# A first and a last group of half the size in a Mamba and dense mixture-of-experts kernel, with the order of its first turns written anew

## The chip, the cores and the metric

The kernel runs on one core of one Trainium2 chip. The core has a matrix engine (PE), a vector engine (DVE), a scalar engine for activations (ACT), a general engine (POOL) and a queue that issues transfers (SP). The time is the device time of one execution in microseconds (us). Before the change it is 934.35 us, the median of three runs (933.2 to 934.37).

## What is computed

Sixteen sequences of 256 tokens, each token a row of 128 numbers, pass through one Mamba block with a small feed-forward network behind it, and then through eight experts of which every one is applied to every token. All numbers are 32-bit floats. Cut to what matters:

```python
# per sequence; D_INNER = 256 (two halves of 128), D_STATE = 16
xi, z = split(layernorm(x, ln1) @ in_proj_w.T)
xc    = silu(causal_conv4(xi) + conv_b)
dt, B, C = split(xc @ x_proj_w.T)                 # 8, 16, 16 columns
dt    = softplus(dt @ dt_proj_w.T + dt_b)
h_t   = exp(dt * A) * h_{t-1} + dt * B * xc        # for each of 256 channels and 16 states
y     = (sum over states of C * h) + D * xc
x1    = x + (y * silu(z)) @ out_proj_w.T
x1    = x1 + relu(layernorm(x1, ln2) @ w1.T + b1) @ w2.T + b2
x2    = layernorm(x + x1)
out   = layernorm(x2 + sum_e (silu(x2 @ Wg[e]) * (x2 @ Wu[e])) @ Wd[e])
```

## The kernel before

**Groups.** The sixteen sequences are taken in groups, `GROUPS = (2,) * 8`: eight groups of two sequences, so 512 token columns each. Channels lie on the 128 partitions, tokens along the free dimension. `W[g]` is the width of a group in columns, `NJ[g]` its number of expert slices; for 512 columns it is 32, one slice for each of 8 experts and 4 blocks of 128 hidden units.

**What one group passes through.** `stage_a` (L339) normalises, transposes, projects (`pi`, L430), convolves on DVE (L443), makes `dt`, `B` and `C` (`pd`, `pv`), writes B and C to DRAM (`bc`, L380, issued by ACT), takes the softplus and forms `u = dt * xc` (L402, on POOL but for one half of group 0). `stage_gate` (L412) makes the gate `zg`. The scan has 32 steps per group, one for each state and each half of the channels. A step is made of: `decay` (L466), an exponential on ACT that writes the factor `dA` into one of `ND` = 3 PSUM banks; `inject` (L479), the product `dBx = B * u` on POOL; `step` (L488), the scan on DVE (L494) and the product `hC` with C (L497), on DVE or, where the order says `p`, on POOL; and `add_state` (L505), which adds `hC` to the sum over states, on POOL (`y`, L523), or, where the order says `e`, on PE into the bank `py` (L521) by a product with the identity. B and C come back from DRAM spread over the partitions by `fetch` (L458), in tiles of two states, two buffers of each, issued by SP. When the last state is added, `yt` is formed (L536) and `stage_c` (L543) follows: the output projection `po` (L551), the sum with x (L558), a normalisation, the feed-forward network `pf` and `pff` (L595, L585), the residual sum `res` (L565, L566, on POOL), a second normalisation, and the transposed result `x2T`. Then the group's expert slices can be worked: `up` (L637) is the product `pg` and its silu, `across` (L646) the product `pu` and the product of both on DVE (L651), `down` (L654) the accumulation `acc` (L667). `stage_e` (L672) closes the group and writes the output. A group of one sequence is handled by the same code: `parts` (L632) puts two (expert, block) pairs of 256 columns into one slice, and `sums` (L499) puts both channel halves into one bank.

**The order.** Nothing is scheduled by a planner at build time: `tc.manual_schedule()` keeps the order in which the code issues instructions, and each engine works its own queue in that order. The order comes from strings of letters. PRE is worked once, then one string of START for each of the first 18 turns, then the 8 strings of TURN over and over. Every letter calls one function, if its condition allows it: L fetches B and C, `s` and `p` are a scan step with the product on DVE or on POOL, `a` and `e` an addition on POOL or PE, `i` inject, `d` decay, `u`, `x`, `w` one slice of up, across, down, and A, B, G, P, C, Z move the running stages by half a step. `m` issues four transposes of the identity into a bank that nothing reads (`busy`, L770), before any expert slice exists.

**Banks and silus.** Four PSUM banks (`NB`) are shared by stages and slices. A stage that takes a bank (`take`, L305) waits in its own program order until fewer than `limit[0]` are held by stages; the limit is `HELD` = (3, 1): three while no slice is ready, one while slices are. Likewise stages that need a silu or softplus on ACT wait, while slices are ready, for the stretch between the letters S and E (`silu_time`, L331).

**Weights.** Before PRE, SP issues the loads of `NEARLY` = 4 experts (L255, three loads of 256 KB for each). The others follow at the beginning of turns 1 to 4 (L799).

**The end.** For the last group `down` splits the accumulation into two parts (`NTAIL` = 2), and holds the last four slices back, so that the two closing stages follow one another.

Of the kernel before, what the change touches and what calls it, by code (L numbers as in the profile page):

```python
# [12 lines left out]
P = 128  # L13
L = 256
# [4 lines left out]
ROW = 32  # L19
KC = 4  # L20
TB = 512
GROUPS = (2,) * 8
NTT = TB // P
NE = 8
NF = 4
# [7 lines left out]
NLATE = 4  # L33
NTAIL = 2
BUFS = 6
HELD = (3, 1)
NB = 4
NEARLY = 4
EPS = 1e-5
FAR = 1e28  # L40
SLOW = 1e-25
# [7 lines left out]


PRE = (
    "L A B A G A L B A G B A A B G m G G A P L L B A A B B L B B "
    "B L P B d d B G B B B A P A A P B G G B L A m L s P d L B L "
    "G A P B A L L L A B A P A A L m i A G A A i G P P G i i G A "
    "B A B A m G m"
)
START = (
    "C i C L L Z m e e a L d C Z p s C s A Z m L s m A s Z i s i "
    "s e",
    "i d e Z A e A A s d s e L C i L Z C m C e A i Z m",  # L60
    "A e C C A i s C C A A C m a Z C e L C d A d A A i A C C e d "
    "e A C L Z A L C s A C",
    "L e d C C Z e e Z A m L d s A Z e s d i i A C C a C s Z A i "
    "L A i i p C d s A s i C L A A d A",
    "L s Z s A m C i L i p s C A i e d d m C L m Z i A L m C C s "
    "i m d d L L L L Z A C C A A e e A C i A C p C e A e m Z C C "
    "Z i",
    "p A A C A A L s C Z d i A d e C d i A C C e A A A A C L i L "
    "A m Z C e e A i L C A C A e m Z a i m C p m s Z m",
    "C s d A A d m A A Z m A i A i i s Z a C L C L m s e C d L A "  # L70
    "Z L C s a C Z L L s A C m L a",
    "A C L d e e e A A m C C a Z A e d i C d i A A C L A A L s e "
    "L C e Z C C A e L s i C L i C m d A d A d C L",
    "L s d A d Z C d C A C s i Z d L i a A d d A d a Z d A A C i "
    "d s A Z L A i C A L i d d C C p C C s C A i C d m C A d A A "
    "C A Z C i L Z a s d Z d i m A",
    "d e C A A p i C p A C s e d L C A A s m L A L a d C C A Z p "
    "C d Z C A A Z m s C L m C Z m Z a d A C C m i d a C",
    "p L A i Z C Z Z s u C i i C Z C p u Z C e x d A i L C x L C "
    "d x C e A C A w p E A C i d i C d Z C w A Z x i C C A Z w S "  # L80
    "C a u C s C C u C L",
    "u d p C w C a C C C C C x i u C m C Z a x p m L C C i i m C "
    "C C w p m C m C x Z i i d i s x E a d C d S Z a u w C L i C "
    "A i",
    "w p u w E p A u Z C m A L A C s C m a S A p Z L s C C d A s "
    "u C A s x m x u A L e s e A m a d A d x A x m A p Z i Z Z A "
    "A w w a d p C A w i C C i",
    "Z x C u w S A m A w Z Z e C s w Z e A A C i w i C s u i A i "
    "u u C L A x A d A Z C x Z L p m L p A A x L C a x Z w A A C "
    "A d C p E C C i",  # L90
    "L L u x Z C A Z C C s u p p i C x C d A Z e u L A w A C d A "
    "L A s C i w e A m A d A C C d C m a C d C Z i L x w C Z C u "
    "s Z w C a C Z C",
    "s i C a i u L w C A L u d L L i S i C A C C x A u A m e i i "
    "C x C e x w m A s C A a u d L C i i w u C A",
    "C s S L e a w a p u i A x A w A A a C C C d Z m u A x d x C "
    "x S C d p C w p E E A x C p Z C A w A A d A C d i Z C Z Z C "
    "m C A d d A C u C S C A C C m C i A m",
    "w C E A C A i A Z C L i C p C A m A w s u u C u x Z w x x a "
    "i d a Z p u w x C A d C L d C i s m E d a C Z L w a i L L A "  # L100
    "u L A",
)
TURN = (
    "w A C Z C s C s i C i Z x C C u s L a u L Z A C x C A A x C "
    "Z Z d C C C C C Z d C a C C w C E d C C L w C w s C A x C d "
    "u L C C C a Z d C C i C u",
    "C u A i w S s u s C i A C a d a Z E Z d A a A x C d C Z a w "
    "C C i C Z A A s C C S C u Z Z x s C C x a d a Z d w d i C A "
    "x d",
    "w u A a s u C C C s C E C L s w A C A u i C a x C A C C A A "  # L110
    "A Z L C C C A S C x w A a C C x C C i C A A S C A i s A Z C "
    "d i E A i C Z C Z i A Z x u C C Z u C Z A C w C A A C",
    "A w C A A a s s C x Z d C A A a d C u w C C a C u w u A E A "
    "A A Z A C a C a i Z s x x L i s s C Z L C u C A Z A C C A x "
    "C w A C A C C C A w A Z A C A C x d L C s C C w Z C a",
    "d s A C A d C u L A C w u C A a x x C A C C a C C x C d A d "
    "C C C s A u i i i A C A",
    "C w C C S a C A x C C u A a A A u s i w s d L w S A a C Z s "
    "C x C C s C C A a C A i a x i d A C A Z A E L L C A w u A C "
    "d",  # L120
    "C A a S C u C S Z u w C w C a A A w s x i u A C C i A u A C "
    "x Z s A A i Z Z C C d a Z x A E A A w L s x C x C A d w s a "
    "w i L C C C i d d C C Z i C i C C a i C d",
    "s A E s C d d Z C u s Z A u C d w s C a C u i x C a A u A w "
    "C x x w A C u d x C w C i A i C C L C u",
)


# [1 line left out]
def kernel(  # L130
# [25 lines left out]
    nc = tc.nc  # L156
    NG = len(GROUPS)
    W = [n * L for n in GROUPS]
    NJ = [NE * NF * w // TB for w in W]
# [12 lines left out]
    def bank(tag, name, bufs=1, w=TB):  # L172
        return ps.tile([P, TB], FP, tag=tag, bufs=bufs, name=name)[:, :w]
# [76 lines left out]
    def load_expert(e):  # L250
        nc.sync.dma_start(out=wg[:, e, :], in_=Wg[e])
        nc.sync.dma_start(out=wu[:, e, :], in_=Wu[e])
        nc.sync.dma_start(out=wd[:, e], in_=Wd[e].rearrange("(f p) d -> p f d", p=P))

    for e in range(NEARLY):  # L255
        load_expert(e)
# [46 lines left out]
    limit = [NB]  # L303
# [25 lines left out]
    silus = [True]  # L329
# [302 lines left out]
    def parts(g, j):  # L632

        n = TB // W[g]
        return [divmod(j * n + i, NF) + (slice(i * W[g], (i + 1) * W[g]),) for i in range(n)]
# [18 lines left out]
    def down(g, j):  # L654
        s = state[g]
        if j == 0:

            n = NTAIL if g == NG - 1 else 1
            s["acc"] = [bank("dA" if i else "acc", f"acc{g}_{i}", ND if i else 1, W[g] // n) for i in range(n)]
        last = g == NG - 1  # L660
        late = last and j >= NJ[g] - NLATE
        if late and j < NJ[g] - 1:
            return
        todo = [p + (s.pop(("h", i)),) for i in range(j - NLATE + 1 if late else j, j + 1) for p in parts(g, i)]
        for part, acc in enumerate(s["acc"]):
            for e, f, cols, h in todo:
                nc.tensor.matmul(  # L667
                    acc, lhsT=wd[:, e, f, :], rhs=h[:, cols][:, bass.ts(part, acc.shape[1])],
                    start=(e == 0 and f == 0), stop=(e == NE - 1 and f == NF - 1),
                )  # L670
# [63 lines left out]
    def step_next(pool=False):  # L734
        t = at["s"]
        if ready(t) and t < at["a"] + BUFS:
            if at["d"] == t:
                decay_next()
            if at["i"] == t:
                inject_next()  # L740
            if at["C"] * NL <= t:
                load_next("C")
            if min(at["d"], at["i"], at["C"] * NL) > t:
                step(t, pool)
                at["s"] += 1
# [19 lines left out]
                    launch("Z", stage_e(g, part, n))  # L765

    def silu(on):
        silus[0] = on or not experts

    def busy():  # L770

# [3 lines left out]
                nc.tensor.transpose(t[:, bass.ts(c, P)], ident, ident)  # L775

    experts = False
    words = dict(
        L=loads, s=step_next, a=add_next, i=inject_next, d=decay_next, u=rise, x=cross, w=lower,
        S=lambda: silu(True), E=lambda: silu(False), m=busy,  # L780
        p=lambda: step_next(True), e=lambda: add_next(True),
    )
# [5 lines left out]
    for word in PRE.split():  # L788
        words[word]()
    assert "ready" in state[0]  # L790
    turn = 0
    while at["w"] < sum(NJ) or any(running.values()):
        assert turn < 2 * NT * NG + len(START)
        experts = at["w"] < len(slices)
        limit[0] = HELD[experts]
        g, k = scans[min(at["a"], len(scans) - 1)]
        if g + 1 < NG and g + 1 not in x_tiles:
            load_x(g + 1)
        if 0 < turn <= NE - NEARLY:  # L799
            load_expert(NEARLY + turn - 1)  # L800
        if k >= START_A * NM and g + 1 < NG and g + 1 not in state and not running["A"]:
            running["A"].append(stage_a(g + 1))
        for word in (START[turn] if turn < len(START) else TURN[(turn - len(START)) % NT]).split():
            words[word]()
            if word == "A":
                half("B")
                half("G")
        turn += 1
# [44 lines left out]
```

## Time and profile before

| what | value |
|---|---|
| median of 3 runs | 934.35 us |
| profiled execution | 933.03 us |
| its span, first to last instruction | 930.9 us |
| granted clock of PE, mean | 0.979 |
| busy PE | 882.6 us (95%) |
| busy DVE, ACT, POOL | 712.4, 711.9, 718.8 us |
| HBM read, written | 76.57 MB, 2.62 MB |
| table loads on ACT | 1283 ns each |
| dBx on POOL (L486), 128x512 | 1275 ns, 256 times |
| additions of y on POOL (L523), 128x512 | 1275 ns, 223 times |
| scan on DVE (L494), 128x512 | 1221 ns, 256 times in all |
| product hC on DVE (L497), 128x512 | 691 ns, 229 times |

The span is what the profile shows; the execution's own time is 2.1 us longer. The busy time of PE includes the letters `m` and modelled ends of products, so that 95% says that its queue is rarely empty, not that it is at its peak. The shares are means over a head, in which there is no expert work yet, a long middle, and an end in which only expert work is left.

### The profile page before, as it was taken

How to read it: one execution, taken by the hardware profiler on the slowest of the kernel's cores; microseconds unless marked ns; L12 is line 12 of the kernel's file. 1: busy time of each engine (PE TensorE's matmuls, PEld its weight loads, DVE VectorE, ACT ScalarE, POOL GpSimd, SP SyncE). 2: the span in 40 equal slices, each digit the busy share in tenths (PEclk: the TensorE clock that was granted, in tenths of full speed). 3: DMA queues.
4: the chain of work that ended last, by engine and by line, in shares of the span. 5: the costliest groups of instructions: out<-in, count | busy, mean ns of one | idle time of the engine just before them, and what ended most of it. 6: DMA issues, size and time to landing. Idle time of an engine off the chain costs nothing. (4 is left out here: it accounts for less than half of the span.)

```text
span 930.9 us, 8897 instructions
## 1 busy us (share of the span) xinstructions
PE 882.6 (95%) x2520; PEld 424.5 (46%) x2520; DVE 712.4 (77%) x1142; ACT 711.9 (76%) x996; POOL 718.8 (77%) x639
## 2 busy tenths in 40 slices
PE   6778797999999999999999999999999999999996
PEld 2334543445444543445344543454444544455564
DVE  4599865676989889988988998988898899723222
ACT  5834588888899799989898889979998889533222
POOL 1799998998999897999799879999799979700000
PEclk9888899999999999999999999999999999999998
DMA  7573411131233221223322223221322222000000
GB/s 203 199 236 137 134 62 68 68 103 57 82 102 110 83 90 60 91 90 102 94 79 90 80 94 101 92 96 53 103 90 92 91 79 90 1 1 11 1 0 12
DMA packets 38129, 79.76 MB, mean 86 GB/s; under 512 B 5936, under 2 KB 19136, under 8 KB 38080
## 3 DMA queue, kind: packets, MB, share of 16 engines
q1 hardware_dynamic: 33456, 76.58, 24.7%
q10 hardware_dynamic: 4624, 2.62, 1.0%
q8 instruction: 20, 0.33, 0.1%
q14 instruction: 29, 0.24, 0.1%
HBM read 76.57 MB, written 2.62 MB: 85 GB/s over the span
## 5 line engine op out<-in xcount | busy, mean ns | idle before, releaser
L486 POOL TENSOR_TENSOR dBx<-B,u 128x512 f32<-128x512 f32 x256 | 320.5, 1275 | 0.0
L494 DVE TENSOR_TENSOR_SCAN dA<-dA,dBx 128x512 f32<-128x512 f32 x229 | 279.7, 1221 | 17.0 <-ACT dA L474 14.0
L523 POOL TENSOR_TENSOR y<-y,hC 128x512 f32<-128x512 f32 x223 | 279.4, 1275 | 0.7 <-DVE hC L497 0.4
L641 PE MATMUL pg<-x2T,wg 128*128 128x512 f32 x512 | 255.7, 601 | 7.3 <-ACT h L643 4.8
L650 PE MATMUL pu<-x2T,wu 128*128 128x512 f32 x512 | 250.8, 595 | 3.3 <-ACT h L643 3.3
L651 DVE TENSOR_TENSOR h<-pu,h 128x512 f32<-128x512 f32 x256 | 170.9, 684 | 107.8 <-PE pu L650 104.8
L667 PE MATMUL acc<-h,wd 128*128 128x512 f32 (+1 forms) x576 | 251.4, 546 | 0.1
L643 ACT ACTIVATE h<-pg 128x512 f32<-128x512 f32 x256 | 147.1, 597 | 114.5 <-PE pg L641 112.4
L474 ACT ACTIVATE dA<-dt,A 128x512 f32<-128x512 f32 x256 | 169.4, 685 | 39.7 <-DVE hC L497 34.3
L497 DVE TENSOR_TENSOR hC<-dA,C 128x512 f32<-128x512 f32 x229 | 158.3, 691 | 18.0 <-POOL y L523 3.5
L667 PEld LDWEIGHTS acc<-h,wd 128*128 128x128 f32 x576 | 107.7, 191 | 110.2 <-issue 100.8
L650 PEld LDWEIGHTS pu<-x2T,wu 128*128 128x128 f32 x512 | 95.7, 190 | 123.0 <-issue 89.9
L641 PEld LDWEIGHTS pg<-x2T,wg 128*128 128x128 f32 x512 | 94.5, 191 | 123.2 <-issue 83.4
L474 ACT ACT_TABLE_LOAD x91 | 116.8, 1283 | 2.4 <-ACT x L291 0.5
L643 ACT ACT_TABLE_LOAD x90 | 115.5, 1283 | 3.3 <-ACT dbc L377 1.8
L283 POOL TENSOR_TENSOR rs_e<-ve_e,mhalf 128x4 f32<-128x4 f32 (+1 forms) x9 | 8.5, 945 | 123.4 <-DVE ve_e L281 123.4
L521 PE MATMUL py<-hC,ident 128*128 128x512 f32 x66 | 39.0, 695 | 9.8 <-DVE hC L497 6.0
L402 POOL TENSOR_TENSOR u<-dt,xc 128x512 f32<-128x512 f32 x15 | 19.5, 1302 | 30.0 <-ACT dt L397 30.0
L494 DVE TENSOR_TENSOR_SCAN hS<-dA,dBx 128x512 f32<-128x512 f32 x27 | 32.3, 1211 | 11.5 <-POOL hC L497 6.5
L443 DVE SCALAR_TENSOR_TENSOR hc<-pi,cw,hc 128x510 f32<-128x510 f32 (+2 forms) x48 | 35.5, 744 | 5.2 <-ACT hc L436 4.1
L497 POOL TENSOR_TENSOR hC<-hS,C 128x512 f32<-128x512 f32 x27 | 34.2, 1271 | 5.4 <-issue 3.2
L585 PEld LDWEIGHTS pff<-w,r 128*128 128x128 f32 x256 | 31.7, 194 | 9.4 <-issue 6.6
(90 smaller groups left out, 612.9 us busy)
## 6 DMA issues: line engine op xcount, KB each, us to landing
B<-bc SPq DMA_DIRECT2D x64, 512.0 KB, 3.8
C<-bc SPq DMA_DIRECT2D x64, 512.0 KB, 4.5
xt<-in_x_dram SPq DMA_DIRECT2D x8, 256.0 KB, 4.4
wg<-in_Wg_dram SPq DMA_DIRECT2D x8, 256.0 KB, 5.1
wu<-in_Wu_dram SPq DMA_DIRECT2D x8, 256.0 KB, 5.4
wd<-in_Wd_dram SPq DMA_DIRECT2D x8, 256.0 KB, 5.9
out_dram<-x ACTq DMA_DIRECT2D x7, 256.0 KB, 4.2
bc<-dbc ACTq DMA_DIRECT2D x8, 64.0 KB, 2.2
```

Of the source, the lines that this page charges most:

```text
L443: nc.vector.scalar_tensor_tensor(hv[:, :, k:], pv[:, :, : L - k], cw[:, h, KC - 1 - k : KC - k], hv[:, :, k:], ALU.mult, ALU.add,)
L474: nc.scalar.activation(s["dA", k], s["dt"][:, h, :], AF.Exp, scale=A_sb[:, h, n : n + 1])
L486: nc.gpsimd.tensor_tensor(s["dBx", k], s["B", k // NL][:, n % NC, :], s["u"][:, h, :], ALU.mult)
L494: nc.vector.tensor_tensor_scan(to, dA, s.pop(("dBx", k)), 0.0, ALU.mult, ALU.add)
L497: engine.tensor_tensor(hC, to, s["C", k // NL][:, k // NH % NC, :], ALU.mult)
L521: nc.tensor.matmul(s["sum", h], lhsT=ident, rhs=hC, start=first, stop=False, skip_group_check=True)
L523: nc.gpsimd.tensor_tensor(y, y, hC, ALU.add)
L641: nc.tensor.matmul(pg[:, cols], lhsT=wg[:, e, bass.ts(f, P)], rhs=s["x2T"], start=True, stop=True)
L643: nc.scalar.activation(s["h", j], pg, AF.Silu)
L650: nc.tensor.matmul(pu[:, cols], lhsT=wu[:, e, bass.ts(f, P)], rhs=s["x2T"], start=True, stop=True)
L651: nc.vector.tensor_mul(s["h", j], pu, s["h", j])
L667: nc.tensor.matmul(acc, lhsT=wd[:, e, f, :], rhs=h[:, cols][:, bass.ts(part, acc.shape[1])], start=(e == 0 and f == 0), stop=(e == NE - 1 ...
```

## The change

The first and the last group become groups of one sequence, 256 columns wide, with seven groups of two between them: nine groups, and 288 scan steps, of which 64 are half as wide. Only two experts are loaded before PRE; six follow at the beginning of turns 1 to 6. In the first 18 turns stages may hold three banks even while slices are ready, and their silus are never held back. `down` no longer removes a slice's h when it uses it, since a slice of a narrow group has two parts. PRE, all of START and all of TURN are written anew.

```diff
-GROUPS = (2,) * 8
+GROUPS = (1, 2, 2, 2, 2, 2, 2, 2, 1)
...
-NEARLY = 4
+NEARLY = 2
...
 PRE = (
-    "L A B A G A L B A G B A A B G m G G A P L L B A A B B L B B "
...
+    "L G i m A i s G B A A m B L B m A A d A B B B A L A d P A L "
...
 START = (
-    "C i C L L Z m e e a L d C Z p s C s A Z m L s m A s Z i s i "
-    "s e",
...
+    "m i A e C L C p A s A A A s L E d C Z s C m C A",
...
 TURN = (
-    "w A C Z C s C s i C i Z x C C u s L a u L Z A C x C A A x C "
-    "Z Z d C C C C C Z d C a C C w C E d C C L w C w s C A x C d "
-    "u L C C C a Z d C C i C u",
...
+    "C w A a C C u u s s Z C C C A s x Z A C C Z A x Z s C A w d "
+    "d a C Z C C w Z C d i C Z Z C d x C x Z w d a u C C d C u C "
+    "u a C",
...
-        todo = [p + (s.pop(("h", i)),) for i in range(j - NLATE + 1 if late else j, j + 1) for p in parts(g, i)]
+        some = range(j - NLATE + 1 if late else j, j + 1)
+        todo = [p + (s["h", i],) for i in some for p in parts(g, i)]
...
     def silu(on):
-        silus[0] = on or not experts
+        silus[0] = on or not experts or turn < len(START)
...
     experts = False
+    turn = 0
...
-    turn = 0
     while at["w"] < sum(NJ) or any(running.values()):
         assert turn < 2 * NT * NG + len(START)
         experts = at["w"] < len(slices)
-        limit[0] = HELD[experts]
+
+        early = turn < len(START)
+        limit[0] = HELD[experts and not early]
+        silus[0] = silus[0] or early
```

## The prediction

> **What bounds the kernel now.** I read the page's busy shares and slices first, then the windows, then the timelines of PE and POOL around three marks: the output projection of a group (`po`, L551), the first expert product of a group (`pg`, L641) and the residual sum of a group on POOL (`res`, L565). A "group" is what one entry of GROUPS gives; g0 is the first.
>
> The slices say that PE is full from about slice 7 on, and POOL nearly full from slice 1 to 34:
>
> ```profile
> PE   6778797999999999999999999999999999999996
> POOL 1799998998999897999799879999799979700000
> ```
>
> Windows (us; then length; then busy us and instruction count of PE, PE loads, DVE, ACT, POOL):
>
> ```profile
> 37.00:94.00 57.00, 46.05 (x147) 21.85 (x145) 54.55 (x61) 27.04 (x38) 54.18 (x47) 0.87 0.55 187
> 94.00:122.00 28.00, 22.02 (x101) 14.51 (x102) 24.36 (x53) 16.99 (x31) 26.41 (x25) 0.85 0.38 121
> 122.00:190.00 68.00, 63.00 (x138) 26.20 (x138) 40.78 (x47) 57.26 (x70) 62.66 (x54) 0.96 0.22 78
> ...
> 503.00:597.00 94.00, 92.91 (x263) 43.11 (x262) 83.36 (x138) 84.21 (x117) 83.26 (x75) 1.00 0.26 85
> ```
>
> Up to about 200 us POOL (with DVE at its side) sets the pace; from then on PE does: 92.9 of 94 us. So the kernel is a head, in which PE lacks work, and a tail of pure PE work, and a change of the head is worth what it moves the moment at which PE runs full. The marks (timelines; start, duration):
>
> ```profile
> 93.38 2.38 PE L551 MATMUL po<-outw,yt 128*128 128x128 f32 x16 [0.58 <-issue]
> 121.61 2.99 PE L641 MATMUL pg<-x2T,wg 128*128 128x512 f32 x4
> 200.36 2.28 PE L551 MATMUL po<-outw,yt 128*128 128x128 f32 x16
> 304.20 2.02 PE L551 MATMUL po<-outw,yt 128*128 128x128 f32 x16
> ...
> 29.29 6.16 POOL L486 TENSOR_TENSOR dBx<-B,u 128x512 f32<-128x512 f32 x5
> 86.41 11.10 POOL L486 TENSOR_TENSOR dBx<-B,u 128x512 f32<-128x512 f32 x9
> 100.49 1.27 POOL L565 TENSOR_TENSOR res<-x,xt 128x512 f32<-128x512 f32 x1
> 206.16 1.27 POOL L565 TENSOR_TENSOR res<-x,xt 128x512 f32<-128x512 f32 x1
> 310.97 1.28 POOL L565 TENSOR_TENSOR res<-x,xt 128x512 f32<-128x512 f32 x1
> ```
>
> Units. In the chain of waits a 512-column expert product (two records) takes 0.86 us of PE ("PE pu L650" 1.72 for x4), and 256 columns take half. POOL back to back gives 11.10 / 9 = 1.23 us for each 512-wide operation. PE's list of a full group, from one po to the next, holds 101.5 us by these units; po2 to po3 in the trace is 405.6 - 304.2 = 101.4. So from po2 on the list itself is the time, and I reckon the end as: **time of po2 plus PE's list behind it.** Before, that is 304.2 + 626.7 = 930.9.
>
> **The change, part by part.** All counts are of the instruction lists of the two built programs, each engine's in its order:
>
> | stretch | POOL before | POOL changed | PE's list before | PE's list changed |
> |---|---|---|---|---|
> | first dBx to res0 | 54 of 512 | 12 of 512, 54 of 256 | | |
> | res0 to res1 (PE: po0 to po1) | 77 of 512 | 61 of 512, 2 of 256 | 89.8 us | 65.7 us |
> | res1 to res2 (PE: po1 to po2) | 73 of 512 | 73 of 512 | 101.5 us | 84.8 us |
> | each later full group | 70 of 512 | 70 of 512 | 101.5 us | 101.5 us |
>
> (POOL has besides some pairs of rs and nb, 1.26 us each, and memsets, 0.3 together.)
>
> *PE behind po2.* The changed list holds 52.2 us more behind po2: 49 expert products not yet done (42.0), the rest projections and feed-forward, since g0 and g1 together are now three sequences of the sixteen, not four. The last group's tail handles 128-column halves, not 256: shorter copy, one transpose, one statistic and one normalisation less in each; from 8.0 us after the last product (922.9 to 930.9) I take off 1.3. So the end is po2 + 626.7 + 52.2 - 1.3 = po2 + 677.6, and **break-even is po2 = 253.3 us**, 51 us earlier than now.
>
> *PRE, up to the first scan.* Following ACT with its own rows (x-norm of half width, 1.28 per table load, softplus 1.06): the first softplus ends at about 23 us (27.3 now), but the new order lets ACT do g1's dbc, a gate and g1's softplus before the first decay: 29.8, first scan about 32 (33.1 now). POOL's queue has both u products of g1 behind its first two dBx, so POOL starts in earnest at 29.8, as now (29.3). A first group of half the width thus gives nothing on POOL up to here.
>
> *g0's scan, POOL.* From the first dBx to res0 POOL has 54 operations of 512 now, in 71.2 us. Changed: 12 of 512 and 54 of 256. No row has a 256-wide product on POOL. Near rows: 4 columns (nb, L285) 201 ns, 512 columns 1275 ns; the line between gives 735 at 256, less the 45 ns by which neighbours overlap: 0.69. Ends: 0.615 (no fixed part) and 0.80. Then 29.8 + 12 x 1.23 + 52 x 0.69 + 1.2 (rs, nb, memsets) = 81.6. DVE's part of it is an estimated 31 us (20 pairs of scan and product, which start 1.93 apart now and would take half of that and the fixed part below, and 12 lone scans), so it waits for POOL; ACT's 32 decays, 0.47 each, are less still.
>
> Two rules of the Trainium skill speak against this part. "VectorE: DVE Perf Modes" (the TRN2 errata section) wants tiles of 512 elements or more, as each instruction pays a fixed time once. The DVE rows have it:
>
> ```profile
> L687 DVE TENSOR_TENSOR x<-pao,x 128x512 f32<-128x512 f32 x7 | 4.8, 682 | 0.5 <-PE pao L298 0.5
> L687 DVE TENSOR_TENSOR x<-pao,x 128x256 f32<-128x256 f32 x2 | 0.8, 422 | 2.9 <-PE pao L298 2.9
> ```
>
> that is 162 ns fixed. The changed list has 90 DVE instructions more: by the rule alone +14.6 us. By the windows DVE has 27 us free in 122 to 190 and 10 in each later 94, and in g0 it waits for POOL: I charge 0 on DVE, and the fixed part only where it is on the path, inside POOL's 0.69. The second: "DMA: Bandwidth & Descriptors" (anatomy of one DMA; measured there for GpSimd's own queue) gives 2.0 us plus bytes at 436 GB/s, so 2.6 us for a B or C block of now 256 KB. The trace's rows on SP's queue: B 3.8 for 512 KB, expert weights 5.1 to 5.9 for 256 KB. A block now lasts some 7 x 0.69 = 4.8 us on POOL and the next-but-one can only be fetched once it is done. By the rule no block is late; by the expert row six blocks could be about 1 late each. NEARLY = 2 puts six experts (4.6 MB) into this same stretch, between the blocks on SP: with B and C 9.3 MB in some 41 us, 227 GB/s, where 37 to 94 now carries 187. I take 2 us (0 to 6.6): **res0 = 83.5**, po0 about 7 earlier (now 100.5 - 93.4), 76.5.
>
> *g0's last stage and first experts.* 28.2 us from po0 to pg0 now. Its parts halve, but the new PE list puts g2's pd and pv and three fillers before the first pg, and g2's whole first stage into ACT: I keep 28, so pg0 at 104.6. The first expert product comes 17 us earlier. The fillers (50 bursts of four for 36) sit where PE waits anyway; those three would cost 0.44 each if it did not.
>
> *res0 to res1, POOL.* Now 77 operations of 512: 94.7 + 4.1 for small ones = 98.8, measured 105.7, so 6.9 idle. Changed: 61 of 512 and 2 halves: 75.0 + 1.4 + 4.1 = 80.5. With an idle between 0 and 6.9 I take 3: 83.5, **res1 = 167**, po1 = 161 (5.8 earlier, as now). PE has only 43.7 us of list between pg0 and po1, for 56 us: g0 now owns 16 slices, and PE runs dry, 12 us.
>
> *res1 to res2.* 73 operations of 512 now and then: 89.8 + 5.3 = 95.1. Now it takes 104.8, because PE's list of 101.5 governs. Changed, PE's list po1 to po2 is only 84.8, so POOL governs: between 95.1 and 101.5 I take 97: **res2 = 264**, po2 = 257 (6.8 earlier, as now). By PE: po1 161 + 28.2 to pg1 + its list of 63.0 = 252: not later.
>
> *The other edits.* Silu stages free and three banks held in the first 18 turns: they show only in the lists' order. ACT gets 11 table loads more (193 to 204; 14.1 us), under ACT's free 11 us in 122 to 190 and 10 in each later 94; between the first normalisations of g1 and g2 it is 26 for 27, so I charge 0; if ACT were late, PE's pg would wait for h. The new TURN: 101.5 us on PE and 70 operations on POOL per group, as before: 0, at most 2 either way.
>
> **Sum.** 257 + 677.6 = 934.6 us of span, against 930.9: +3.7. Outside the span lie 2.1 us (933.03 - 930.9), and the median of the runs is 1.3 above the profiled one: **938.0 us**. PE begins with experts 17 us earlier and loses more than that by waiting for POOL twice.
>
> **Rivals.**
> - *Faster: POOL's half-width operations are cheap and it never idles.* 0.615, no late block, no idle: res0 77.8, res1 158, res2 253, po2 246.4 (by PE 243.5): span 924, **927.4 us**. It decides as soon as po2 is before 253.3, that is if my three stretches together are 4 us shorter. For it: POOL idles only 4 us in 30 to 130 now. Against: the 201 ns of a 4-wide operation, and 6.9 idle in the next stretch.
> - *Faster by far: PE governs, POOL keeps up.* pg0 104.6 + 43.7 + 28.2 + 63.0 = po2 239.5, **920.5 us**. It needs res0 to res1 in 71 us, and 61 x 1.23 is 75 already.
> - *No change that can be measured* (within 0.2%, about what a measurement of this kernel can tell): po2 between 251.4 and 255.2.
> - *Much slower: SP's queue.* Experts between the blocks make each block late (6.6 us, res0 88), and both later stretches have the idle of now (87.4, 101.5): res2 277, po2 270, **951 us**. For it: 227 GB/s and in-order issue. Against: peaks over 340 GB/s in the present head.
>
> **How the numbers follow.** Forecast (slower by 0.2 to 1%) 0.45; much slower 0.17; no change 0.13; first rival 0.21; second 0.04. So faster 0.25, same 0.13, slower 0.62. Taking the unknown half-width price, the DMA wait and the two idles to their likely ends, po2 lies between 245 and 267: 926 to 948 us.
>
> **What will show it.** Right: res0 near 83, pg0 near 105, PE idle between pg0 and po1 and again before pg1, res1 to res2 near 97 with POOL over 95% busy, po2 near 257, and 677 us from po2 to the end. Wrong: 256-wide dBx far from 0.735; B landing late and DVE or POOL waiting on a DMA in 35 to 75 us; po2 before 253; a po-to-po period other than 101.5 later on.

## The result and the profile after

The changed kernel takes **970.28 us** (median of 3 runs, 970.23 to 970.98) where the kernel before takes 934.35: a ratio of 1.0391, 95% interval 1.0367 to 1.0415. The forecast was 938.0 with a range of 926 to 948. The direction was right and the size was not. The profiled execution has a span of 969.2 us, 34.6 more than the 934.6 reckoned.

The marks of the prediction first, from the timelines of the changed kernel: `po` (output projection of a group, PE L551) and `res` (residual sum, POOL L565). Each row has start, duration, and the instructions merged into it; a row has fewer than a group's 16 (or 8) products where the view ended or the products came in two parts.

```profile
77.48 1.05 PE L551 MATMUL po<-outw,yt 128*128 128x128 f32 x8
162.38 0.38 PE L551 MATMUL po<-outw,yt 128*128 128x128 f32 x2
268.58 1.59 PE L551 MATMUL po<-outw,yt 128*128 128x128 f32 x10
375.00 2.28 PE L551 MATMUL po<-outw,yt 128*128 128x128 f32 x16
481.44 2.27 PE L551 MATMUL po<-outw,yt 128*128 128x128 f32 x16
587.85 2.26 PE L551 MATMUL po<-outw,yt 128*128 128x128 f32 x16
694.27 2.30 PE L551 MATMUL po<-outw,yt 128*128 128x128 f32 x16
...
83.91 0.74 POOL L565 TENSOR_TENSOR res<-x,xt 128x256 f32<-128x256 f32 x1
169.22 1.26 POOL L565 TENSOR_TENSOR res<-x,xt 128x512 f32<-128x512 f32 x1
276.82 1.28 POOL L565 TENSOR_TENSOR res<-x,xt 128x512 f32<-128x512 f32 x1
```

Up to 170 us the forecast holds: po0 77.5 for 76.5, res0 83.9 for 83.5, po1 162.4 for 161, res1 169.2 for 167. Then two things go wrong. From po1 to po2 it takes 106.2 us where 96 were reckoned, so that po2 comes 11.6 late. And from po2 on each group takes 106.4 us, four times running and to within 0.03, where PE's list holds 101.5. Of the 34.6 us too many, 11.6 lie before po2, 19.7 in the four periods from po2 to po6 (425.7 for 406.0), and the last 3.3 behind po6.

The windows of one such period, before and then after (us, length, busy us and instruction count of PE, PE loads, DVE, ACT, POOL, then the granted clock, the DMA share and GB/s):

```profile
508.07:609.98 101.91, 100.82 (x281) 46.71 (x281) 90.37 (x145) 91.73 (x128) 91.17 (x81) 1.00 0.27 89
```

```profile
481.44:587.85 106.41, 102.32 (x282) 46.48 (x281) 91.86 (x146) 90.85 (x127) 91.39 (x81) 1.00 0.26 85
```

The reader is to see that no engine has more to do: the counts agree to one, the clock is full in both, and DVE, ACT and POOL are busy as long as before. PE's record is 1.5 us longer. One more product in the record (0.43) and the products that had waited, each recorded some 0.1 longer (1.13 for 1.02 us for a pair), make up over half of that; the rest is not accounted for. PE's idle grows from 1.1 to 4.1 us. So 4.5 us are lost with equal work. The timeline of PE shows where; in brackets, how long PE stood idle and who ended it. First all waits of over 0.25 us in this period of the kernel before, then the four longest of the changed kernel:

```profile
508.82 1.83 PE L551 MATMUL po<-outw,yt 128*128 128x128 f32 x14 [0.28 <-POOL yt L536]
563.07 1.98 PE L641 MATMUL pg<-x2T,wg 128*128 128x512 f32 x4 [0.27 <-DVE h L651]
566.28 1.13 PE L641 MATMUL pg<-x2T,wg 128*128 128x512 f32 x2 [0.38 <-ACT h L643]
```

```profile
506.83 1.13 PE L650 MATMUL pu<-x2T,wu 128*128 128x512 f32 x2 [0.93 <-DVE h L651]
541.72 1.13 PE L650 MATMUL pu<-x2T,wu 128*128 128x512 f32 x2 [0.65 <-ACT dt L393]
543.63 1.12 PE L641 MATMUL pg<-x2T,wg 128*128 128x512 f32 x2 [0.78 <-ACT h L643]
558.51 1.13 PE L641 MATMUL pg<-x2T,wg 128*128 128x512 f32 x2 [0.88 <-ACT h L643]
```

An expert product writes into one of four PSUM banks. Here it waits until the bank's last reader is done: the silu (`h`, ACT L643), the product of `h` (DVE L651) or the bias of `dt` (ACT L393). Each of these stands in its own engine's queue behind whatever the strings of TURN have put there.

The chain of waits of this page reaches back only to 671 us, so it doesn't tell what sets a period; the experiments have to.

In the stretch res1 to res2 it is POOL that waits. Window, then POOL's, DVE's and ACT's timelines:

```profile
169.22:276.82 107.60, 96.06 (x268) 46.04 (x269) 86.48 (x134) 88.62 (x123) 94.65 (x84) 0.95 0.25 83
```

```profile
177.19 1.27 POOL L497 TENSOR_TENSOR hC<-hS,C 128x512 f32<-128x512 f32 x1 [2.91 <-issue]
183.36 1.27 POOL L497 TENSOR_TENSOR hC<-hS,C 128x512 f32<-128x512 f32 x1 [3.44 <-DVE hS L494]
205.36 0.71 POOL L283 TENSOR_TENSOR rs_e<-ve_e,mhalf 128x2 f32<-128x2 f32 x1 [3.29 <-DVE ve_e L281]
...
175.83 1.22 DVE L494 TENSOR_TENSOR_SCAN hS<-dA,dBx 128x512 f32<-128x512 f32 x1 [2.50 <-ACT dA L474]
182.06 1.22 DVE L494 TENSOR_TENSOR_SCAN hS<-dA,dBx 128x512 f32<-128x512 f32 x1 [3.51 <-ACT dA L474]
...
174.46 0.69 ACT L599 ACTIVATE r<-pf,fb 128x512 f32<-128x512 f32 x1 [2.16 <-PE pf L595]
175.04 0.68 ACT L474 ACTIVATE dA<-dt,A 128x512 f32<-128x512 f32 x1
```

Read it upwards from the end. POOL's product hC waits for a scan on DVE, the scan for a decay on ACT, and the decay is queued behind g1's feed-forward `r`, which waits for PE. POOL is busy 94.65 us, just what was reckoned (95.1), but it is idle 13, not 2. The two waits for `hC` are 6.4 us of the 13; another 3.3 is a wait for the statistics `ve_e`.

### The profile page after: what moved, and what is told of

Read it like the earlier page. It is cut to its first block, busy times and chain, and to the rows that moved or that the text cites. A ratio compares the mean times of both kernels' runs of the same rounds, so it can differ in the third digit from the quotient of the medians.

```text
span 969.2 us, 9802 instructions
## 1 busy us (share of the span) xinstructions
PE 891.3 (92%) x2796; PEld 458.9 (47%) x2796; DVE 737.1 (76%) x1225; ACT 737.2 (76%) x1059; POOL 735.5 (76%) x715
## 5 line engine op out<-in xcount | busy, mean ns | idle before, releaser
L486 POOL TENSOR_TENSOR dBx<-B,u 128x512 f32<-128x512 f32 (+1 forms) x288 | 327.9, 1157 | 22.5 <-DVE dA L494 20.9
L523 POOL TENSOR_TENSOR y<-y,hC 128x512 f32<-128x512 f32 (+1 forms) x253 | 295.8, 1186 | 19.1 <-DVE hC L497 18.9
L494 DVE TENSOR_TENSOR_SCAN dA<-dA,dBx 128x512 f32<-128x512 f32 (+1 forms) x263 | 293.7, 1117 | 19.3 <-ACT dA L474 17.6
L641 PE MATMUL pg<-x2T,wg 128*128 128x512 f32 (+1 forms) x576 | 257.3, 558 | 16.6 <-ACT h L643 11.0
L650 PE MATMUL pu<-x2T,wu 128*128 128x512 f32 (+1 forms) x576 | 254.6, 550 | 10.9 <-DVE h L651 4.6
L651 DVE TENSOR_TENSOR h<-pu,h 128x512 f32<-128x512 f32 x256 | 172.0, 685 | 113.5 <-PE pu L650 86.2
L668 PE MATMUL acc<-h,wd 128*128 128x512 f32 (+2 forms) x640 | 255.7, 508 | 1.0 <-DVE h L651 1.0
L643 ACT ACTIVATE h<-pg 128x512 f32<-128x512 f32 x256 | 145.1, 596 | 99.0 <-PE pg L641 95.0
L474 ACT ACTIVATE dA<-dt,A 128x512 f32<-128x512 f32 (+1 forms) x288 | 177.3, 637 | 55.1 <-DVE hC L497 48.6
L497 DVE TENSOR_TENSOR hC<-dA,C 128x512 f32<-128x512 f32 (+1 forms) x263 | 168.0, 639 | 24.8 <-DMA C<-bc 4.5
L650 PEld LDWEIGHTS pu<-x2T,wu 128*128 128x128 f32 x576 | 105.2, 191 | 116.9 <-issue 71.4
L443 DVE SCALAR_TENSOR_TENSOR hc<-pi,cw,hc 128x510 f32<-128x510 f32 (+5 forms) x54 | 36.7, 685 | 7.2 <-ACT hc L436 6.0
L776 PE MATMUL busy<-ident 128*128 128x128 f32 x200 | 35.5, 306 | 2.9 <-POOL mhalf L216 1.4
```

Source lines behind the costliest of these rows:

```text
L443: nc.vector.scalar_tensor_tensor(hv[:, :, k:], pv[:, :, : L - k], cw[:, h, KC - 1 - k : KC - k], hv[:, :, k:], ALU.mult, ALU.add,)
L474: nc.scalar.activation(s["dA", k], s["dt"][:, h, :], AF.Exp, scale=A_sb[:, h, n : n + 1])
L486: nc.gpsimd.tensor_tensor(s["dBx", k], s["B", k // NL][:, n % NC, :], s["u"][:, h, :], ALU.mult)
L494: nc.vector.tensor_tensor_scan(to, dA, s.pop(("dBx", k)), 0.0, ALU.mult, ALU.add)
L497: engine.tensor_tensor(hC, to, s["C", k // NL][:, k // NH % NC, :], ALU.mult)
L523: nc.gpsimd.tensor_tensor(y, y, hC, ALU.add)
```

## Experiments

All ratios are to the kernel before, run on the same chip beside it, with the 95% interval. A "period" is from one po to the next between po2 and po6.

**Old TURN in the changed kernel.** All eight strings are those of before:

```diff
 TURN = (
-    "C w A a C C u u s s Z C C C A s x Z A C C Z A x Z s C A w d "
+    "w A C Z C s C s i C i Z x C C u s L a u L Z A C x C A A x C "
...
```

> The changed kernel with the eight strings of TURN of before; all else as changed. Theory T (the new TURN's order loses some 5 us per group, because products of experts stand behind a bank that ACT frees late): later periods from po to po fall from 106.4 to 101.5-103 us, the time from 970.3 to 938-950. Rival H (what loses the time is that a half group has shifted everything against everything else, whatever the strings): periods stay near 106, time 965-975. Rival B (order of the first turns and TURN fit together and old strings fit the new head worse): over 975.

Measured 977.63 us, 1.0466 (1.0451 to 1.0482): theory T fails as it was put, and B comes closest. Periods fall, but only to 104.6, and po1 to po2 rises from 106.2 to 114.4. In the kernel before the same strings give 101.9. The same strings are not the same order, though. A letter does nothing where its condition fails, so what is issued depends on the state in which a string begins. In one period some 16 of PE's 280 instructions stand elsewhere than in the kernel before. And the experts are two slices further behind. Call the silus of earlier groups that are still to be done at a po the backlog, counted in ACT's timeline: it is ten at each po from po2 to po6, and eight in the kernel before. So a string has no period of its own; the state in which it begins counts.

**New TURN in the kernel before.** The same edit the other way round.

> The kernel before with the eight strings of TURN of the change; all else as before. Theory T: periods of 106 us in place of 101.4, seven of them, so 934.4 + about 25 to 35 = 958-970. Rival H: periods stay at 101-102, 932-938.

Measured 956.28 us, 1.0228 (1.0207 to 1.0248), periods of 106.4. The old groups, with all else of the head, lose 22 us by the strings alone. PE's timeline shows the very waits of the changed kernel, at the same distance from po (25.4, 60.3, 62.2 and 77.0 us behind 521.36):

```profile
546.73 1.13 PE L651 MATMUL pu<-x2T,wu 128*128 128x512 f32 x2 [0.93 <-DVE h L652]
581.62 1.13 PE L651 MATMUL pu<-x2T,wu 128*128 128x512 f32 x2 [0.65 <-ACT dt L394]
583.53 1.13 PE L642 MATMUL pg<-x2T,wg 128*128 128x512 f32 x2 [0.78 <-ACT h L644]
598.41 1.13 PE L642 MATMUL pg<-x2T,wg 128*128 128x512 f32 x2 [0.88 <-ACT h L644]
```

The lists agree too. From po to po the instructions of PE, DVE, ACT and POOL (280, 145, 126 and 80) stand by name in the very order of the changed kernel, and in both the backlog is nine. Equal order and equal backlog gave an equal period, with a first group of either width. With these strings the half group has no part in the 106.4 (rival H is out for them).

**Without the rule for the first 18 turns.**

```diff
-        early = turn < len(START)
-        limit[0] = HELD[experts and not early]
-        silus[0] = silus[0] or early
+        limit[0] = HELD[experts]
...
-        silus[0] = on or not experts or turn < len(START)
+        silus[0] = on or not experts
```

> The changed kernel without the rule for the first 18 turns (three held banks, silu free); all else as changed. If the three held banks starve the experts in the first turns (a theory for the 11.6 us that po1 to po2 took more than predicted), po2 falls from 268.6 to about 257 and the time to about 959. If the rule costs nothing or gains, po2 stays or gets later (the lists of PE up to po2 are 3 us shorter without it), and the time is 965 to 985. Later periods 106.4 in both.

Measured 992.57 us, 1.0625 (1.0609 to 1.064): the rule doesn't starve the experts, it is worth 22 us. Without it po1 to po2 is 115.0 and the periods are 107.6, although the rule no longer acts there and not a letter of TURN differs. As with the old TURN, what differs is the state: from po3 on the backlog is eleven, for nine, and some 16 of PE's 280 instructions stand elsewhere.

**The groups alone**, in the kernel before, with its own PRE, START, TURN and NEARLY:

```diff
-GROUPS = (2,) * 8
+GROUPS = (1, 2, 2, 2, 2, 2, 2, 2, 1)
```

> The kernel before with GROUPS of the change (first and last group of one sequence) and nothing else that matters: PRE, START, TURN, NEARLY of before. Theory T: later periods about 101.5, so the time is po2 + 678; the old strings were not written for a narrow first group, so po2 is 255 to 270 and the time 935 to 950. Rival H: periods of 104 to 107, time over 955.

Measured 981.16 us, 1.0505 (1.0489 to 1.0521). Periods are 104.2, within rival H's bounds, and po2 is at 292.8, far behind the 255 to 270 that theory T expected. So with the old strings the narrow group does cost 2.3 us in each period (2.7 with all else as changed), and much at the head: break-even was 253.3. Either narrow groups cost this under any order, or an order loses when it meets a shift that it wasn't written for. The trace speaks for the second. From po to po all four engines have their instructions, by name, in the order of the kernel before, but the experts are one slice ahead: the backlog is seven, for eight. So PE is through with a group's slices one slice sooner, and has two waits in each of the four periods that the kernel before doesn't have, for the next group's `x2T` and for ACT's copy `ao` of the finished sum:

```profile
530.79 1.12 PE L641 MATMUL pg<-x2T,wg 128*128 128x512 f32 x2 [1.12 <-ACT x2T L625]
541.18 1.12 PE L668 MATMUL acc<-h,wd 128*128 128x512 f32 x2 [0.68 <-ACT ao L681]
```

**One pair of waits taken away.** In the changed kernel, TURN only: a store's last steps go from the end of string 1 into string 2.

```diff
-    "u A C d x C d d C C Z w C A a x Z a",
+    "u A C d x C d d C C w C A a x a",
-    "a A C C C A s u C A S w x C C a C A A x u C C S C w L u S i "
+    "a A C C C A s u C A S w x C C a C A A x u C C S C w L u Z Z S i "
```

> The changed kernel; in TURN the two steps of the group before's last stage (its normalisation on ACT, 4 operations and 1.65 us, and the issue of its store on ACT's queue, 0.4 us) move from the end of string 1 to string 2 behind the softplus. Theory P (the period is 106.4 and not 101.5 because at a few places ACT or DVE reaches the silu or the product of h that frees a PSUM bank too late): the two waits of PE at 541.7 (0.65, for ACT dt) and 543.6 (0.78, for ACT h) go, with the some 0.26 that each matmul after a wait takes longer; a period of 104.4 to 104.8, the time 957-962. Rival L (ACT's and DVE's lists as a whole set the pace, so that a wait taken away comes back elsewhere): a period above 105.8, the time 966-971.

Measured 974.77 us, 1.0433 (1.0409 to 1.0457): no gain. The waits at 541.7 and 543.6 have indeed gone, and the periods are 106.2, 106.2, 107.9 and 105.9. Of the two others shown above, the 0.93 is as it was (at 403.64, behind the po at 378.27) and the other has doubled:

```profile
455.16 1.13 PE L642 MATMUL pg<-x2T,wg 128*128 128x512 f32 x2 [1.82 <-ACT h L644]
```

ACT's timeline fits this: the normalisation and the store that were moved now stand before the next run of silus and decays.

```profile
443.49 1.64 ACT L292 ACTIVATE x<-x,nb_e,rs_e 128x128 f32<-128x128 f32 x4
445.16 0.40 ACTq L696 DMA_DIRECT2D out_dram<-x  x1
445.59 1.28 ACT L475 ACT_TABLE_LOAD   x1 [0.46 <-ACT x L292]
446.88 1.30 ACT L475 ACTIVATE dA<-dt,A 128x512 f32<-128x512 f32 x2
...
449.50 1.09 ACT L644 ACTIVATE h<-pg 128x512 f32<-128x512 f32 x2
...
454.51 1.09 ACT L644 ACTIVATE h<-pg 128x512 f32<-128x512 f32 x2
```

The silus at 449.5 and 454.5 are where they were behind their po (71.2 and 76.2 us here, 71.4 and 76.4 in the changed kernel). So PE came earlier and waited longer, and its idle in the period only fell from 4.1 to 3.9 us. (The 0.26 us that the expectation adds for a product after a wait is 0.1 in the rows.) A wait on PE is thus not always a loss that can be taken off by itself. The Trainium skill ("Perfetto Trace Analysis", section Optimization Strategy) has the reader find the gaps on the engine that is to be filled and make what they wait for start sooner; done here for two gaps of 1.43 us together, it left the period at 106.2 for 106.4.

**Two further places**, as well: in string 3 two scan steps and a decay (`s d` and `s`) go behind the third product of gates, in string 7 the residual add goes behind two products of h.

```diff
-    "s w C Z A C C A x w s d A a u A s u x C C Z C C u a A C x w "
+    "s w C Z A C C A x w A a u A u x C C Z C C u s d s a A C x w "
...
-    "A i s A d s i A C A u w u C w i C C d s C d A L L d a s C d "
-    "x x C i C u C u x i w Z C L C x w A u u",
+    "A i s A d s i A C A u w u C w i C C d s C d A L L d a s d "
+    "x x C C i C u C u x i w Z C L C x w A u u",
```

> As the kernel with the store later, and two further places of TURN: in string 3 the two decays that split four silus (two table loads of 1.28 each between them) go behind the third product of gates, and in string 7 the step that puts DVE's residual add and statistics (2.1 us) ahead of two products of h goes behind these. Theory P: the waits of 0.88 and 0.93 go as well; a period of 102 to 103, the time 942-950. Rival L: still above 105.5, 964-971.

Measured 1007.61 us, 1.0793 (1.0772 to 1.0813), periods of 112.5. Both of the waits aimed at went, and others came: 2.13 us of `pu` for DVE's h, 1.72 of `px` for the normalisation on ACT, 1.69 of `po` for POOL's yt. Both theories missed it; that the later scans and the later x2T hold these up is likely, but was not tried singly.

**Decays early in START**, TURN untouched. Five letters are put in (two scan steps, two decays, one dBx), none is taken out behind for them, and one `e` goes:

```diff
     "m i C i S s L A C i d x L C a a Z x A s E A d u C m i C d A "
-    "a C A C Z C a L A C w x A m A d C e E C C Z C a d s C d m d "
+    "a s d C A C p d i Z C a L A C w x A m A d C E C C Z C a d s C d m d "
```

> The changed kernel; in START string 16 two scan steps and two decays of g2 (and one dBx) move ahead of g1's normalisation and feed-forward, where ACT is idle 4.1 us before 169.3; one word that would have taken a bank for sums is left out. TURN as changed. Theory Q (the 11.6 us that po1 to po2 took beyond the prediction are POOL idle: its products hC wait for scans on DVE, these for decays on ACT, these for g1's feed-forward): POOL's idles of 2.9 and 3.4 us at 177 and 183 go, po2 falls from 268.6 to 261-264, the time to 963-966. Rival (PE's or ACT's list governs that stretch, and POOL's idle is slack): po2 within 1.5 of 268.6, 968.5-972. Periods of 106.4 in both.

Measured 1049.37 us, 1.1242 (1.1224 to 1.1261). The stretch res1 to res2 does fall, from 107.6 to 102.3: the idle of 2.9 us has gone and the one of 3.4 is 1.9. But res1 is 3 us later, so po2 gains only 1.9. And every period after it is 119.6 to 119.9, with not one letter of TURN changed. Counted in DVE's timeline, two more scans are done at each expert product than in the changed kernel, from the head to the last full group. PE's timeline in such a period, at its longest waits:

```profile
534.83 2.05 PE L585 MATMUL pff<-w,r 128*128 128x128 f32 x16 [1.34 <-ACT r L599]
545.22 1.63 PE L298 MATMUL px<-ident,x 128*128 128x128 f32 x4 [3.16 <-ACT x L291]
```

So the state in which START hands over to TURN acts on all periods behind it.

**Both edits together.**

> The edits of the three places in TURN and of the decays in START together. Theories P and Q: the sum of the two gains, 934-944, still not below the kernel before. If one takes the other's gain: 945-960.

Measured 1082.55 us, 1.161 (1.1582 to 1.1638), periods of 124.5 to 126.1 us. The losses add up, near enough (112 us over the changed kernel, 37 and 79 apart); the gains expected never came.

After these there is a new theory. With the engines 85 to 96% busy, each in its own fixed order, a period is as long as the longest ring of waits that leads through several engines back to itself one group later. Then the letters, the state at turn 18 and the groups are one thing and can't be costed apart, and a wait on PE is only where the ring passes PE. To test it, the lists of all engines were reckoned through with the durations of the trace's rows and the waits between them, and letters moved so that the reckoned end came early. ("Fitted" below means this.)

**TURN fitted to the changed head.** GROUPS, PRE, START, NEARLY and the rule are as changed; all eight strings of TURN are new. String 4:

```diff
-    "w A a u u C s x E d Z A C Z x C C C A i d a L C C A s i d C "
-    "L x d",
+    "i E w A i a C A C u s A a u C x L Z Z d E L x A C Z d A a A "
+    "L w C d i Z C S Z s C",
```

> The changed kernel, all but the eight strings of TURN as changed. The strings are fitted anew: each engine's list was reckoned through with the durations of the trace's rows and the waits between the lists, and letters moved until the end came earliest (reckoned: 957.7 as changed, 930.2 so, and 927.6 for the kernel before; periods 105.1, 100.5 and 102.0). Theory C (a period is the longest ring of waits through PE, ACT, DVE and POOL; the order of the letters alone makes it 106.4, and the head with its narrow group does not stand against 101.5): periods of 101 to 102.5, the time 936-948. Rival H (a first group of half the width keeps the experts so short of stock that no order reaches 101.5): periods of 104 or more, the time 955 or more.

Measured 947.9 us, 1.015 (1.0129 to 1.017), periods of 102.3. Of the 36 us lost, 22 come back by order alone, with the narrow groups in place. One period in the windows, and all of PE's waits of over 0.25 us in it:

```profile
472.96:575.25 102.29, 100.96 (x282) 46.70 (x281) 91.95 (x146) 91.74 (x128) 91.25 (x81) 1.00 0.27 88
```

```profile
497.32 1.12 PE L651 MATMUL pu<-x2T,wu 128*128 128x512 f32 x2 [0.34 <-DVE h L652]
529.50 1.13 PE L651 MATMUL pu<-x2T,wu 128*128 128x512 f32 x2 [0.83 <-ACT dt L394]
```

The same 282 PE records and the same work on DVE and POOL as at 106.4, with the narrow groups: rival H is out here too. Still po2 is at 268.4, for START was not touched. The reckoning itself was 18 us too early (930.2).

**TURN fitted in the kernel before**, in the same manner.

> The kernel before, with TURN alone fitted in the same way (reckoned 917.1 against 927.6, periods 99.9 against 102.0). If the reckoning holds for a kernel whose PE is full, periods near 100.5-101.5 and the time 920-928; if PE's list of 101.5 us per group is all there is, 931-936.

Measured 933.38 us, 1.0003 (0.9994 to 1.0012): nothing. Periods are 101.2 for 101.9, not the 99.9 reckoned; and the 2.7 us gained in the four periods from po2 to po6 are lost again in the next (97.4 for 94.0). Where PE is already full, this other order of TURN gave nothing.

**START and TURN fitted, groups as changed.** The last open step of the prediction was whether the narrow head can give what was reckoned for it.

```diff
-    "A L A e s Z C A C A L m e C L s e A s i Z C L d C C Z e i A "
-    "i i L L C L d e C Z i m e",
+    "i s s p i s d x w A s a A A Z i C d u m C E e e Z p u Z E u "
+    "S Z A i L e i L e C e",
```

(START string 6; the other strings of both likewise.)

> GROUPS, PRE, NEARLY and the rule for the first 18 turns as changed; START and TURN both fitted anew in the same manner (reckoned with a matmul of 0.866 us and 0.09 us from an instruction's end to the start of one that waits for it: 920.8; by the same numbers 972.0 as changed, 939.8 for the kernel before; po2 at 247.5, periods 100.9). Theory O (the narrow group is as good as the prediction's best cases, and what lost 36 us is the order alone): po2 at 248-255, periods 101-102, the time 922-935, at or below the kernel before. Rival N (half-width groups cost something at the head that no order removes): po2 later than 260, the time over 940.

Measured **929.85 us**, 0.9953 (0.9939 to 0.9967): 40 us below the changed kernel with the same groups, rule and PRE, and 0.5% below the kernel before. Its marks, and the window of res1 to res2:

```profile
75.59 1.18 PE L551 MATMUL po<-outw,yt 128*128 128x128 f32 x8
162.12 1.95 PE L551 MATMUL po<-outw,yt 128*128 128x128 f32 x16
258.80 1.95 PE L551 MATMUL po<-outw,yt 128*128 128x128 f32 x16
```

```profile
168.80:266.73 97.93, 92.28 (x268) 45.59 (x268) 90.62 (x137) 84.61 (x120) 93.34 (x84) 0.98 0.24 83
```

From po1 to po2 it takes 96.7 us (reckoned in the prediction: 96), po2 is at 258.8 (257), and a period is 101.1 on the mean (101.5). POOL is idle 4.6 us in res1 to res2, not 13. So the times that the prediction reckoned for these stretches can be reached with these groups, with this order. The 247.5 expected for po2 was missed by 11, so the gain over the kernel before is small.

**START and TURN fitted, groups as before.**

> The kernel before with START and TURN both fitted in the same manner (reckoned 919.8, po1 at 191.7 for 201.3). If the old groups gain as much by it as the new ones, 921-930, and the regrouping as such is worth nothing; if the new ones are below it by over 3 us, the regrouping has a gain of its own.

Measured **920.14 us**, 0.9858 (0.9844 to 0.9873), po1 at 195.8 for 200.4 and the periods 101.0 on the mean. It is the fastest of all, and 9.7 us below the narrow groups fitted in the same manner. With a fresh order on either side, the regrouping as such showed no gain. The two orders need not be equally good, though: this end was reckoned to 0.3 us (919.8), that of the narrow groups 9 us too early (920.8), which is nearly the whole difference. How far a better order for the narrow groups might still go isn't known.

## Why the prediction was wrong

- *"PE's list, po2 + 677.6."* The reckoning as such held only where the order let PE run full: 700.6 us behind po2 in the changed kernel, 677.3 (945.6 - 268.35) with TURN fitted, 671.0 with both fitted. Why the last is 6.6 below the sum was not traced.
- *"The new TURN: 101.5 us on PE and 70 operations on POOL per group, as before: 0, at most 2 either way."* **This is the step that failed.** Equal lists were taken for equal time. The step measured 4.9 us in each period, 19.7 in the four from po2 to po6, and the same strings put alone into the kernel before cost 22. (The title names the first turns only, but the eight strings that work every later group are new as well.) What failed is the step from list to time, not just the choice of the new strings over the old: with the old ones the changed kernel has periods of 104.6 and is slower still. The prediction named the wait ("if ACT were late, PE's pg would wait for h") and the sign to watch ("a po-to-po period other than 101.5"), yet compared ACT's load with its free time only, not with its order, and gave the sign no rival and no share of the range. Its unit was checked on the shortest of the four periods, 101.4; their mean before is 101.9.
- *"Between 95.1 and 101.5 I take 97"* for res1 to res2. This is the second step that failed, and it put po2 11.6 us late. The work was right (94.65 busy), the idle was not: 13 us for 2. POOL's products hC hang on decays that the new START queues on ACT behind g1's feed-forward. With both fitted it is 97.9, so the value was possible and the order missed it.
- *PRE and g0's scan.* POOL starts in earnest at 29.98 (29.8 predicted). The half-width operation, which no row of before showed, takes 0.73 us recorded and 0.70 in a row (0.735 and 0.69). The line drawn between two sizes came out:

```profile
45.32 3.48 POOL L486 TENSOR_TENSOR dBx<-B,u 128x256 f32<-128x256 f32 x5
```

- *"I take 2 us" for late blocks, and the rival with SP's queue.* A median B block of 256 KB landed after 3.4 us and C after 3.8; the estimate from the figure of the Trainium skill ("DMA: Bandwidth & Descriptors", anatomy of one DMA), which is for GpSimd's queue, is 2.6. DVE did wait 4.5 us for C blocks in 35 to 75 us, one of the signs named. But POOL waited for a DMA only 0.3 us in 30 to 110, and res0 came at 83.9 for 83.5. The rival's 951 us had another reason behind it than what came.

```profile
B<-bc SPq DMA_DIRECT2D x16, 256.0 KB, 3.4
C<-bc SPq DMA_DIRECT2D x16, 256.0 KB, 3.8
```

- *"I keep 28, so pg0 at 104.6."* It came at 109.44, 32 us behind po0. By itself that moved nothing that was late: po1 followed POOL, 1.4 us behind the forecast.
- *"The other edits ... show only in the lists' order"*, at nothing. True in the letter, but the order was the price. The rule for the first 18 turns is worth 22 us with these strings, as taking it away shows.
- *PE waits twice for POOL*, the reason given for "slower": right in kind. The first stretch, res0 to res1, had POOL idle 5.4 us for 3 predicted; the second is told above. That the direction was right was partly luck: most of the loss came from the step above, which was set at 0, and with both orders fitted the same groups are 0.5% faster than before.

What is shown: the strings alone cost 22 us with the old groups, another order alone gives back 22 us with the new ones, then 18 more with START fitted too, and equal lists in equal order with an equal backlog had equal periods. What is argued: that a ring of waits through several engines sets a period. Its consequences were seen (a wait removed on PE without gain, the period altered from START alone, equal work at 101.1 to 125 us), the ring itself no view of the profile shows. Which letters carry the 4.9 us was not isolated; the attempts by hand, at one place and at three, gained nothing or made it worse. NEARLY and PRE were not tried alone.

## What to carry to other kernels

Where several engines are each over 85% busy in a fixed order, as here, equal instruction counts need not mean equal time: a rewritten order is a change of its own, and it should get a price, a rival and a share of the range, the larger the more of it is new. Before an order is believed, list for each scarce buffer who frees it and what is queued before that reader on its engine. Such a list names the waits, not what taking one away is worth: two attempts of that kind gained nothing here. To tell order from size, compare the engines' lists one instruction after another, and count how far one stage stands behind another. In this case a change of sizes could be judged only after the order had been fitted to it and to the old sizes alike; before that the comparison was one of orders.

## What the runs showed beside this

The order of the head acts on the whole run: a handover two scan steps further on made each of the four periods after it some 119.7 us instead of 106.4, though the same eight strings repeat. Of 1.4 us of idle taken from PE at two places, most came back at another within the same period. And the changed kernel's period repeats to 0.03 us over four groups: whatever loses the time is set by the order, not by chance or by the clock, which was 1.00 in these windows.
